# Three small attentions issued in groups of two or three pairs of tiles, with a group's products in one row

## The chip, the cores and the metric

The program runs on one core of a Trainium2 chip. A core has five engines that run their own instruction streams side by side and meet at semaphores: the matrix engine (TensorE, PE in the profile; its weight loads are shown as PEld), the vector engine (VectorE, DVE), the scalar engine (ScalarE, ACT), GpSimd (POOL) and SyncE (SP). Data moves between memory and the core's buffer by DMA transfers that an engine's queue issues. Matmul results land in eight accumulation banks of 128 partitions by 512 f32 values.

The metric is the time of one execution of the whole program in device microseconds (us).

## The reference

The reference is a residual network of sixteen layers over x of shape (16, 256, 128), in f32: each layer adds its output for the normed x to x. The order is: a linear attention with a running error, a local attention, a performer attention, the local attention again, a linear attention with a convolution, a layer of eight experts of which two are taken for each token, a decay attention, the experts again, a causal linear attention, a channel mix, a window attention with its own experts, the mix again, a rotary attention, an adapter layer of experts, a state-space layer and the adapters again.

The change touches three of them, each with 16 heads of 8 dimensions over 256 tokens. Cut to what they compute:

```python
def decay(x):                     # every pair of tokens
    scores = einsum('bqhd,bkhd->bhqk', q, k) * 8**-0.5
    scores = scores * exp(-alpha * abs(i - j))
    return einsum('bhqk,bkhd->bqhd', softmax(scores), v) @ Wo.T + bo

def causal_linear(x):             # key not after query, no softmax
    q, k = relu(q) + 1e-6, relu(k) + 1e-6
    out = einsum('bhnd,bhnde->bhne', q, cumsum(einsum('bhnd,bhne->bhnde', k, v)))
    return (out / max(scale * position, 1e-6)) @ proj.T

def rope(x):                      # key not after query
    q, k = rotate(q), rotate(k)   # real halves kept, the others set to 0
    scores = where(causal, q @ k.T * 8**-0.5, -1e10)
    return (softmax(scores) @ v) @ Wo.T + bo

x = x + layer(layernorm(x))       # sixteen times
```

## The kernel before, in words

x stays on the core as 128 channels by 4096 tokens, cut into 8 chunks of 512 tokens. A chunk holds two sequences (b = 0, 1), and a sequence has two tiles of 128 tokens. A pair of tiles is (it, jt): query tile and key tile. The softmax is taken without subtracting a maximum; `guard` records the largest entries of queries and keys, and another program is run in the end if they are too large.

The three stages `decay` (L2905), `rope` (L2978) and `causal_linear` (L3025) give their own parts to one shared routine, `small_stage` (L2766). Each names its pairs in `units`: decay has four per sequence ((0,0) and (1,1) with a decay table, (0,1) and (1,0) with a decay that is folded into queries and keys beforehand as `qx` and `kx`), causal_linear two ((0,0) and (1,1); the pair between them is carried by a sum over the first tile), rope three ((0,0), (1,0) and (1,1)). An item is one pair of one sequence of one chunk; decay has 64 items, eight a chunk, causal_linear 32, rope 48.

An item's work on PE has two parts, and the array is cut differently for them:

- `score(n)` (L2783): four row-tiled matmuls (32 rows each; the masked queries of four heads side by side as moving data) into four banks. They are evicted into a score buffer `pt` of 128 by 2048 f32: in decay by four table multiplies on DVE, then an exp over the whole buffer on ACT in the next slot; in decay's other kind and in rope by four exps on ACT, for rope's diagonal pairs then a mask on DVE in the next slot; in causal_linear by masks on DVE and copies on ACT with masks on POOL.
- `weigh_by_head` (L2818; decay and rope) or `weigh` (L2797; causal_linear): 16 column-tiled products (32 columns each, 128 by 128) into one bank.

Everything else on PE uses the whole array: the norm of the chunk (`norm_x_step`, three steps), the projections, the values, and after the last product of a query tile in decay and rope `raw` (a copy out of the bank: by ACT for tile 0, by DVE for tile 1), `turn` (L2839: four transposes and a division by the sum), `join` (L2854: two transposes back and a copy into `ot`), `out` (L2865: the output projection, added to x). In causal_linear `finish` takes the place of raw, turn and join. After `out` come the steps that lead into the next layer (`lead`, L1831): for causal_linear and rope the next norm, where it is taken over; for decay the eight steps of the sending to the experts: three of the norm, `compare` (the router's matmul and a comparison, on PE, DVE and POOL), `choose` (DVE, POOL), `place`, `turn` (transposes, two copies on ACT) and `scatter` (L3620), which issues eight indirect DMAs from POOL's queue. The expert stage's first fetch waits for the last scatter.

The order of all of this is written out by hand: under `manual_schedule` each engine gets its instructions in the order in which the Python code issues them. The loop goes over slots n, one item a slot. In a slot it issues the score of item n, then what is due in this slot (the rest of the last eviction, lead steps, turn, join), then an output projection if one is ready, then the products of item n − 3 (`lag = 3`), then the steps of `steps` whose offset falls on this slot. An offset counts slots from the chunk's first score: (−6, project) is six slots ahead of it. `masked_copy` (L2894) makes the masked queries `qz` by two DVE and two ACT operations. Eight banks are split into six for scores and whole-array work and two for products; there are four `pt` buffers.

Helpers that record instructions, so that many operations share a line: `mm` L503, `tr` (transposes) L507, `act` L527, `tt` (DVE) L530, `gt` (POOL) L533, `ts` L537 and L539, `stt` L542, `copy_out` L638.

Of the kernel before, what the change touches and what calls it, by code (L numbers as in the profile page):

```python
# [11 lines left out]
F32, BF16, I32 = mybir.dt.float32, mybir.dt.bfloat16, mybir.dt.int32  # L12
# [1636 lines left out]
class Fast(Net):  # L1649
# [1116 lines left out]
    def small_stage(self, w, units, steps, tiles, evict, finish=None):  # L2766

        nc = self.nc
        lag = 3
        with ExitStack() as st:
            p = self.stage(st, "sm", 1)
            items = [(c, b, *u) for c in range(NCH) for b in range(2) for u in units]
            pts, po, ots, os, later, due = {}, {}, {}, {}, [], {}
            lead = self.lead(p, "s")
            first = min(at for at, _ in steps) - 4  # L2780
            steps = [(first + i, lambda c, i=i: self.norm_x_step(p, c, i, "s")) for i in range(3)] + list(steps)

            def score(n):  # L2783
                c, b, it, jt, kind = items[n]
                k, q, _ = tiles(c, b, it, jt)
                pt = p.tile([P, 4, 4, P], F32, tag="pt", name="pt", bufs=4)
                ps = []
                for r in range(4):
                    rows = slice(32 * r, 32 * r + 32)
                    ps.append(self.bank("s"))  # L2790
                    self.mm(ps[r].rearrange("p (h t) -> p h t", h=4), k[rows], q[rows])
                rest = evict(kind, pt, ps)
                if rest:
                    due.setdefault(n + 1, []).append((lambda _: rest(), None))
                pts[n] = pt

            def weigh(n):  # L2797
                c, b, it, jt, kind = items[n]
                vz = tiles(c, b, it, jt)[2]
                if n % len(units) == 0:  # L2800
                    po[0] = self.bank("o")
                pt = pts.pop(n)
                first, last = n % len(units) == 0, n % len(units) == len(units) - 1
                for u in range(4):
                    for r in range(4):
                        cc = slice(32 * r, 32 * r + 32)
                        nc.tensor.matmul(
                            po[0][cc, it * P : it * P + P], vz[:, u, cc], pt[:, r, u], start=first and u == 0,
                            stop=last and u == 3, skip_group_check=True,
                        )  # L2810
                if last:
                    if b == 0:
                        ots[c] = p.tile([P, CH], F32, tag="ot", name="ot", bufs=2)
                    finish(c, b, ots[c][:, b * T : b * T + T], po[0])
                    if b == 1:
                        later.append(c)

            def weigh_by_head(n, slot):  # L2818
                c, b, it, jt, kind = items[n]
                vo = tiles(c, b, it, jt)[2]  # L2820
                mine = [i for i, u in enumerate(units) if u[0] == it]
                first, last = n % len(units) == mine[0], n % len(units) == mine[-1]
                if first:
                    po[it] = self.bank("o")
                pt = pts.pop(n)
                for u in range(4):
                    for r in range(4):
                        nc.tensor.matmul(
                            po[it][32 * r : 32 * r + 32, u * P : u * P + P], vo[:, 4 * r + u], pt[:, r, u],
                            start=first and u == 0, stop=last and u == 3, skip_group_check=True,  # L2830
                        )
                if last:
                    raw = p.tile([P, CH], F32, tag="raw", name="raw", bufs=2)
                    self.copy_out(it, raw, po.pop(it))
                    due.setdefault(slot + 1, []).append((lambda n: turn(n, raw), n))
                    if it:
                        due.setdefault(slot + 2, []).append((join, n))

            def turn(n, raw):  # L2839
                c, b, it, *_ = items[n]  # L2840
                pt = self.bank("s")
                for u in range(4):
                    self.tr(pt[:, u * P : u * P + P], raw[:, u * P : u * P + P])
                src = pt.rearrange("p (u r d) -> p u r d", u=4, r=4)
                rd = p.tile([P, 4, 4], F32, tag="rd", name="rd", bufs=2)
                nc.vector.reciprocal(rd, src[:, :, :, 8])
                o = p.tile([P, P], F32, tag="o", name="o", bufs=3)
                self.tt(
                    o.rearrange("p (r u d) -> p u r d", r=4, u=4), src[:, :, :, :8],
                    rd[:, :, :, None].broadcast_to([P, 4, 4, 8]), ALU.mult,  # L2850
                )
                os[c, b, it] = o

            def join(n):  # L2854
                c, b, *_ = items[n]
                if b == 0:
                    ots[c] = p.tile([P, CH], F32, tag="ot", name="ot", bufs=2)
                pt = self.bank("s")
                for it in range(2):
                    self.tr(pt[:, it * P : it * P + P], os.pop((c, b, it)))  # L2860
                self.act(ots[c][:, b * T : b * T + T], pt[:, :T], AF.Copy)
                if b == 1:
                    later.append(c)

            def out(c):  # L2865
                pz = self.bank("s")
                self.mm(pz, w["Wo"], ots.pop(c))
                x = self.x[:, self.chunk(c)]
                if "bo" in w:
                    self.stt(x, pz, w["bo"], x, ALU.add, ALU.add)  # L2870
                else:
                    self.tt(x, x, pz, ALU.add)

            with self.share(s=6, o=2), self.tc.manual_schedule():
                self.logs()
                many = 2 * len(units)
                for n in range(first, len(items) + lag + (1 if finish else 3) + len(lead)):
                    if 0 <= n < len(items):
                        score(n)
                    for f, c in due.pop(n, []):  # L2880
                        f(c)
                    if later:
                        c = later.pop()
                        out(c)
                        for i, f in enumerate(lead):
                            due.setdefault(n + 1 + i, []).insert(0, (f, c))
                    if lag <= n < len(items) + lag:
                        weigh(n - lag) if finish else weigh_by_head(n - lag, n)
                    for at, f in steps:
                        c, u = divmod(n - at, many)  # L2890
                        if u == 0 and 0 <= c < NCH:
                            f(c)

    def masked_copy(self, pool, q, b):  # L2894

# [9 lines left out]
    def decay(self, w):  # L2905
# [4 lines left out]
        with ExitStack() as st:  # L2910
# [34 lines left out]
            def queries(c, b):  # L2945
                qzs[c, b] = self.masked_copy(p1, qs[c], b)
# [5 lines left out]
            def queries_by_edge(c, b):  # L2952
                qxs[c, b] = p1.tile([P, 4, T], F32, tag="qx", name="qx", bufs=3)
                self.gt(qxs[c, b], qzs[c, b], edge[:, None, :].broadcast_to([P, 4, T]), ALU.mult)
# [7 lines left out]
            def tiles(c, b, it, jt):  # L2962
# [2 lines left out]
                return kk[c][:, j : j + P], qq[c, b][:, :, it * P : it * P + P], vzs[c % 2][:, 2 * b + jt]  # L2965

            steps = [
                (1, guard), (-6, project), (-5, values), (-4, lambda c: queries(c, 0)), (-3, keys_by_edge),
                (-2, lambda c: queries_by_edge(c, 0)), (0, lambda c: queries(c, 1)), (2, lambda c: queries_by_edge(c, 1)),
            ]  # L2970
            units = [(0, 0, 0), (0, 1, 1), (1, 1, 0), (1, 0, 1)]
            self.small_stage(w, units, steps, tiles, evict)
# [5 lines left out]
    def rope(self, w):  # L2978
        h0 = self.ha
        nc = self.nc  # L2980
        with ExitStack() as st:
# [28 lines left out]
            def queries(c, b):  # L3010
                qzs[c, b] = self.masked_copy(p1, held[c, "q"], b)

            def tiles(c, b, it, jt):
# [1 line left out]
                return held[c, "k"][:, j : j + P], qzs[c, b][:, :, it * P : it * P + P], vzs[c % 2][:, 2 * b + jt]  # L3015

            steps = [
                (0, lambda c: self.guard(ROPE, c, held[c, "q"], held[c, "k"])),
                (-5, lambda c: turned(c, "q")), (-4, lambda c: turned(c, "k")), (-2, values),
                (-3, lambda c: queries(c, 0)), (-1, lambda c: queries(c, 1)),  # L3020
            ]
            units = [(0, 0, 1), (1, 0, 0), (1, 1, 1)]
            self.small_stage(w, units, steps, tiles, evict)
# [1 line left out]
    def causal_linear(self, w):  # L3025
# [3 lines left out]
        with ExitStack() as st:  # L3029
# [46 lines left out]
            def queries(c, b):  # L3076
                qzs[c, b] = self.masked_copy(p1, qs[c], b)
# [24 lines left out]
            def finish(c, b, o, po):  # L3102
# [3 lines left out]
                self.gt(o[:, P:], cross, rd[:, P:], ALU.mult)  # L3106

            steps = [
                (-5, project), (-4, first_tiles), (-3, lambda c: queries(c, 0)), (-2, values),
                (-2, summed), (-1, lambda c: queries(c, 1)), (0, crossed),  # L3110
            ]
            self.small_stage(w, [(0, 0, 0), (1, 1, 0)], steps, tiles, evict, finish)

# [609 lines left out]
```

## Time and profile before

| | us |
|---|---|
| median of 3 runs | 4578.29 |
| lowest and highest | 4572.87, 4580.91 |
| the profiled execution's own time | 4623.81 |
| its span on the core | 4621.7 |
| PE busy (share of the span) | 4064.9 (88%) |
| DVE busy | 2502.5 (54%) |
| ACT busy | 2349.6 (51%) |
| POOL busy | 1946.4 (42%) |

The granted clock of TensorE is 0.943 of full speed over the span. The profile is one execution and stands 45.5 us above the median of the timed runs. In it the decay stage lies at 2315 to 2632 us from the start, causal_linear at 2858 to 2992, rope at 4003 to 4223. Lines of a timeline give the start, the duration, the engine, the line of the kernel, the operation, the tile written and the tile read; "32*128" is a row-tiled, "128*32" a column-tiled and "128*128" a whole-array matmul; x8 means that eight such instructions were put together. What stands in brackets is the idle time before, with what ended it.

### The profile page before, as it was taken

What the parts mean: (1) busy time and instruction counts of PE and PEld (TensorE: products, weight loads), DVE (VectorE), ACT (ScalarE), POOL (GpSimd) and SP (SyncE); (2) the same over time, 40 slices, a digit from 0 to 9 for tenths busy, and PEclk for the clock granted to TensorE, in tenths of its full rate; (3) what the DMA queues carried; (4) which work ended last, traced back from release to release, by engine and by line L of the source; (5) the groups of instructions that cost most, each with busy time, mean ns of one, the idle gap of its engine ahead of it and who ended that gap; (6) DMA issues with size and microseconds to landing.
All of it is one profiled execution on the core that took longest, in us unless ns stands there. A gap on an engine that the chain in (4) does not pass through costs nothing. (4 is left out here: it accounts for less than half of the span.)

```text
span 4621.7 us, 71773 instructions
## 1 busy us (share of the span) xinstructions
PE 4064.9 (88%) x28232; PEld 2185.1 (47%) x28232; DVE 2502.5 (54%) x4453; ACT 2349.6 (51%) x4425; POOL 1946.4 (42%) x1784
## 2 busy tenths in 40 slices
PE   6899999999899999957988698979998888898868
PEld 2455455574455455436744386533333333444323
DVE  4764665462665576462365434635656566476454
ACT  6665465446665466532376433454444443664432
POOL 4653454232654354144434344644433366421241
PEclk9999999999999999978999799989999989999979
DMA  1800000000000000015400162000000000000000
GB/s 55 317 1 1 10 1 1 18 1 1 19 1 1 3 2 1 1 32 173 142 7 15 58 194 78 18 15 1 1 1 1 3 1 0 14 1 17 6 0 19
DMA packets 73081, 142.36 MB, mean 31 GB/s; under 512 B 11007, under 2 KB 42373, under 8 KB 72609
## 3 DMA queue, kind: packets, MB, share of 16 engines
q1 hardware_dynamic: 57120, 114.46, 7.5%
q0 software_dynamic: 9088, 16.94, 1.1%
q10 hardware_dynamic: 6528, 6.29, 0.4%
q8 instruction: 226, 3.70, 0.3%
q14 instruction: 119, 0.97, 0.1%
HBM read 84.22 MB, written 55.25 MB: 30 GB/s over the span
## 5 line engine op out<-in xcount | busy, mean ns | idle before, releaser
L527 ACT ACTIVATE pt<-ps 128x512 f32<-128x512 f32 (+1 forms) x896 | 420.2, 537 | 300.4 <-PE ps L503 296.3
L503 PE MATMUL ps<-hb,w 128*128 128x512 f32 (+1 forms) x960 | 482.4, 630 | 27.7 <-DVE hb L542 21.6
L503 PE MATMUL ps<-w,hb 128*128 128x512 f32 (+2 forms) x896 | 416.0, 578 | 18.7 <-DVE t L530 11.6
L530 DVE TENSOR_TENSOR t<-ps,tab 128x512 f32<-128x512 f32 x512 | 319.2, 683 | 195.9 <-ACT sq L527 192.1
L533 POOL TENSOR_TENSOR t<-t,ss 128x1024 f32<-128x1024 f32 x128 | 243.5, 1902 | 312.4 <-ACT ss L527 203.6
L533 POOL TENSOR_TENSOR t<-t,t 128x512 f32<-128x512 f32 x256 | 320.1, 1272 | 13.1 <-PE ps L503 10.1
L503 PEld LDWEIGHTS ps<-hb,w 128*128 128x128 f32 (+1 forms) x960 | 180.5, 197 | 306.5 <-issue 245.8
L533 POOL TENSOR_TENSOR nsq<-ha 128x512 f32<-128x512 f32 x128 | 141.8, 1108 | 362.2 <-ACT ha L527 338.9
L503 PE MATMUL ps<-nsq,ct 128*128 128x512 f32 x368 | 214.8, 668 | 80.3 <-POOL nsq L533 62.2
L530 DVE TENSOR_TENSOR u<-u,ps 128x512 f32<-128x512 f32 x220 | 129.2, 591 | 227.8 <-PE ps L503 157.2
L527 ACT ACTIVATE pt<-pt 128x768 f32<-128x768 f32 (+1 forms) x160 | 170.1, 1063 | 156.3 <-DVE pt L530 156.3
L503 PE MATMUL ps<-ot,w 128*128 128x512 f32 x448 | 211.1, 607 | 28.5 <-ACT ot L527 21.8
L2182 POOL DMA_INDIRECT back<-y,x x156 | 152.5, 978 | 198.0 <-ACT y L527 169.3
L530 DVE TENSOR_TENSOR ot<-ps,rd 128x512 f32<-128x512 f32 (+1 forms) x208 | 136.3, 655 | 177.4 <-ACT rd L527 142.0
L503 PE MATMUL ps<-qkt 64*128 64x192 f32 (+1 forms) x2048 | 217.3, 328 | 11.8 <-ACT pt L527 11.8
L503 PE MATMUL ps<-u,w 128*128 128x512 f32 (+1 forms) x448 | 221.7, 618 | 5.9 <-POOL u L533 5.9
L503 PE MATMUL ps<-xt,w 128*128 128x256 f32 x936 | 220.4, 386 | 3.6 <-DMA w<-in_moe_x 2.6
L503 PEld LDWEIGHTS ps<-qkt 64*128 64x128 f32 x2048 | 154.2, 189 | 135.6 <-ACT qkt L527 51.5
L503 PEld LDWEIGHTS ps<-w,hb 128*128 128x128 f32 x896 | 148.1, 193 | 143.3 <-issue 103.0
L527 ACT ACTIVATE nrs<-ps,ct 128x512 f32<-128x512 f32 x208 | 140.1, 685 | 146.1 <-PE ps L503 143.2
L530 DVE TENSOR_TENSOR pt<-ps,w 128x384 f32<-128x384 f32 (+1 forms) x320 | 171.1, 575 | 76.0 <-PE ps L503 72.6
L527 ACT ACTIVATE rd<-rd 128x256 f32<-128x256 f32 x256 | 106.7, 417 | 207.6 <-DVE rd L530 201.4
(359 smaller groups left out, 8840.4 us busy)
## 6 DMA issues: line engine op xcount, KB each, us to landing
w<-in_moe_x SPq DMA_DIRECT2D x78, 533.0 KB
rows<-t SPq DMA_DIRECT2D x64, 520.0 KB
x<-rows SPq DMA_DIRECT2D x78, 130.0 KB
w<-in_local_f SPq DMA_DIRECT2D x8, 659.5 KB
y<-back ACTq DMA_DIRECT2D x16, 256.0 KB
y<-back SPq DMA_DIRECT2D x16, 256.0 KB
w<-in_local_f SPq DMA_DIRECT2D x4, 658.5 KB
back<-y,x POOLq DMA_INDIRECT x156
```

The costliest lines, as they stand in the source:

```text
L503: self.nc.tensor.matmul(out, lhsT, rhs, start=start, stop=stop)
L527: self.nc.scalar.activation(out, in_, func, **kw)
L530: self.nc.vector.tensor_tensor(out, a, b, op)
L533: self.nc.gpsimd.tensor_tensor(out, a, b, op)
L2182: nc.gpsimd.indirect_dma_start(views[2 * i + t], bass.IndirectOffsetOnAxis(ap=x[:, t, C : C + 1].bitcast(I32), axis=0), y[:, t], None, bou ...
```

## The change

- A group is two slots where the number of pairs is even (decay, causal_linear) and three in rope.
- The products of a group's items are no longer issued one a slot, three slots behind the score. They are all issued in the last slot of the next group, one after the other, behind that slot's score.
- Due work no longer goes into any slot: `later` puts it into slots that are not the last of their group (with groups of two, every second slot). Turn comes one such slot after the products, join two, out three (causal_linear: out one), and the lead steps in the slots after that, one in each. The three norm steps stand a group apart.
- What is due in a slot is issued in reverse order of its entry; the rest of the eviction comes first, the stage's own steps come ahead of the products instead of behind them.
- Score buffers: 2 × group, four as before in decay and causal_linear, six in rope.
- Offsets of the stages' own steps move so that they fall on slots that are not the last of a group; in decay keys_by_edge goes from −3 to −2, beside queries_by_edge of sequence 0.

```diff
-        lag = 3
+        many = 2 * len(units)
+        group = 2 if len(units) % 2 == 0 else 3
...
-            first = min(at for at, _ in steps) - 4
-            steps = [(first + i, lambda c, i=i: self.norm_x_step(p, c, i, "s")) for i in range(3)] + list(steps)
+            first = min(at for at, _ in steps) - 3 * group
+            steps = [(first + i * group, lambda c, i=i: self.norm_x_step(p, c, i, "s")) for i in range(3)] + list(steps)
+
+            def later(n, i, f, c):
+
+                for _ in range(i):
+                    n += 1 if n % group < group - 2 else group - n % group
+                due.setdefault(n, []).append((f, c))
...
-                pt = p.tile([P, 4, 4, P], F32, tag="pt", name="pt", bufs=4)
+                pt = p.tile([P, 4, 4, P], F32, tag="pt", name="pt", bufs=2 * group)
...
-                rest = evict(kind, pt, ps)
-                if rest:
-                    due.setdefault(n + 1, []).append((lambda _: rest(), None))
+                rests[n] = evict(kind, pt, ps)
...
-                        later.append(c)
+                        later(slot, 1, out, (slot, c))
...
-                    due.setdefault(slot + 1, []).append((lambda n: turn(n, raw), n))
+                    later(slot, 1, lambda n: turn(n, raw), n)
                     if it:
-                        due.setdefault(slot + 2, []).append((join, n))
+                        later(slot, 2, join, (slot, n))
...
-                    later.append(c)
+                    later(slot, 3, out, (slot, c))
...
+                for i, f in enumerate(lead):
+                    later(slot, (2 if finish else 4) + i, f, c)
...
-                many = 2 * len(units)
-                for n in range(first, len(items) + lag + (1 if finish else 3) + len(lead)):
+                n = first
+                while n < len(items) + group or due:
                     if 0 <= n < len(items):
                         score(n)
-                    for f, c in due.pop(n, []):
+                    if rest := rests.pop(n - 1, None):
+                        rest()
+                    for f, c in reversed(due.pop(n, [])):
                         f(c)
-                    if later:
-                        c = later.pop()
-                        out(c)
-                        for i, f in enumerate(lead):
-                            due.setdefault(n + 1 + i, []).insert(0, (f, c))
-                    if lag <= n < len(items) + lag:
-                        weigh(n - lag) if finish else weigh_by_head(n - lag, n)
                     for at, f in steps:
                         c, u = divmod(n - at, many)
                         if u == 0 and 0 <= c < NCH:
                             f(c)
+                    if n % group == group - 1:
+                        for i in range(n - 2 * group + 1, n - group + 1):
+                            if 0 <= i < len(items):
+                                weigh(i, n) if finish else weigh_by_head(i, n)
+                    n += 1
...
             steps = [
-                (1, guard), (-6, project), (-5, values), (-4, lambda c: queries(c, 0)), (-3, keys_by_edge),
-                (-2, lambda c: queries_by_edge(c, 0)), (0, lambda c: queries(c, 1)), (2, lambda c: queries_by_edge(c, 1)),
+                (-6, project), (-4, values), (-4, lambda c: queries(c, 0)), (-2, keys_by_edge),
+                (-2, lambda c: queries_by_edge(c, 0)), (0, lambda c: queries(c, 1)), (0, guard), (2, lambda c: queries_by_edge(c, 1)),
             ]
...
             steps = [
-                (0, lambda c: self.guard(ROPE, c, held[c, "q"], held[c, "k"])),
-                (-5, lambda c: turned(c, "q")), (-4, lambda c: turned(c, "k")), (-2, values),
-                (-3, lambda c: queries(c, 0)), (-1, lambda c: queries(c, 1)),
+                (-6, lambda c: turned(c, "q")), (-5, lambda c: turned(c, "k")), (-3, values), (-2, lambda c: queries(c, 0)),
+                (0, lambda c: queries(c, 1)), (1, lambda c: self.guard(ROPE, c, held[c, "q"], held[c, "k"])),
             ]
...
             steps = [
-                (-5, project), (-4, first_tiles), (-3, lambda c: queries(c, 0)), (-2, values),
-                (-2, summed), (-1, lambda c: queries(c, 1)), (0, crossed),
+                (-6, project), (-4, first_tiles), (-4, lambda c: queries(c, 0)), (-2, values),
+                (-2, summed), (0, lambda c: queries(c, 1)), (0, crossed),
             ]
```

## The prediction

> **What bounds the kernel now.** I read the view by stretches of time first, over the three stages that the change touches (decay, causal_linear, rope, in this order), then over single chunks of them, from one output projection to the next. Columns: the stretch and its length, busy time (instructions) of PE, PEld, DVE, ACT and POOL, the granted clock, the DMA share, GB/s.
>
> ```profile
> 2315.00:2632.00 317.00, 259.07 (x3028) 140.23 (x3026) 178.47 (x447) 193.80 (x306) 116.10 (x110) 0.90 0.05 15
> 2858.00:2992.00 134.00, 129.36 (x1531) 70.89 (x1532) 97.71 (x208) 68.43 (x138) 87.55 (x90) 0.99 0.01 2
> 4003.00:4223.00 220.00, 196.99 (x2245) 103.91 (x2246) 159.44 (x212) 137.84 (x281) 48.86 (x27) 0.96 0.01 1
> 2344.58:2371.66 27.08, 26.59 (x362) 14.09 (x358) 17.50 (x35) 21.17 (x34) 6.00 (x3) 1.00 0.01 2
> 2407.34:2447.12 39.78, 32.50 (x387) 17.68 (x383) 21.70 (x55) 24.81 (x40) 15.44 (x15) 0.91 0.05 15
> 2900.37:2918.87 18.50, 18.26 (x199) 9.66 (x199) 12.81 (x28) 10.22 (x20) 12.32 (x13) 1.00 0.00 1
> 4099.12:4127.80 28.68, 26.25 (x287) 13.15 (x287) 21.05 (x28) 18.86 (x38) 8.69 (x5) 1.00 0.01 1
> ```
>
> The three stages are 671 of 4621.7 us. PE is the fullest engine in each: causal_linear's chunk is PE alone (18.26 of 18.50); rope leaves 2.4 us of 28.68; decay's first chunks are full (26.59 of 27.08), but from the third on, where the sending to the experts (scatters) runs beside the attention, a chunk takes 40 us with 7 idle.
>
> Next the timeline of PE in causal_linear: start, length, line, operation, array tile. Row groups (32*128) are scores, column groups (128*32) products, 128*128 whole-array work.
>
> ```profile
> 2851.55 1.88 PE L503 MATMUL ps<-ha,w 128*128 128x512 f32 x4
> 2853.27 0.94 PE L503 MATMUL ps<-w,ha 128*128 128x128 f32 x7
> ...
> 2912.12 1.14 PE L503 MATMUL ps<-qz,k 32*128 32x512 f32 x8
> 2913.19 1.13 PE L503 MATMUL ps<-nsq,ct 128*128 128x512 f32 x2
> 2914.24 1.08 PE L2807 MATMUL ps<-pt,vz 128*32 128x128 f32 x32
> 2915.25 1.14 PE L503 MATMUL ps<-qz,k 32*128 32x512 f32 x8
> 2916.32 1.08 PE L2807 MATMUL ps<-pt,vz 128*32 128x128 f32 x32
> 2917.34 0.94 PE L503 MATMUL ps<-w,ha 128*128 128x128 f32 x6
> ```
>
> Two projections of 512 columns in one mode start 1.72 us apart, 0.86 each. The same work takes 1.07, 1.05, 1.01, 1.07, 1.02 start to start where the mode changes. So a change costs: rows to whole 0.21, whole to columns 0.19, columns to rows 0.15, rows to columns 0.21, columns to whole 0.16; 0.18 on average.
>
> Then decay's fifth chunk on POOL and PE, the place of the idle time:
>
> ```profile
> 2504.92 1.06 POOL L3624 DMA_INDIRECT rows<-out,idx  x1 [5.27 <-ACT out L527]
> 2506.28 0.96 POOL L3624 DMA_INDIRECT rows<-out,idx  x1 [0.30 <-issue]
> ...
> 2513.85 0.96 POOL L3624 DMA_INDIRECT rows<-out,idx  x1 [0.30 <-issue]
> 2514.83 1.27 POOL L533 TENSOR_TENSOR kx<-k,edge 128x512 f32<-128x512 f32 x1
> ...
> 2526.64 2.36 POOL L533 TENSOR_TENSOR qx<-qz,edge 128x1024 f32<-128x1024 f32 x1
> ```
> ```profile
> 2517.05 1.12 PE L507 MATMUL ps<-ct,raw 128*128 128x128 f32 x4 [5.70 <-ACT raw L527]
> 2518.10 1.94 PE L2828 MATMUL ps<-pt,vo 128*32 128x128 f32 x32
> 2519.97 1.84 PE L503 MATMUL ps<-qz,k 32*128 32x512 f32 x8
> ```
> ```profile
> ACT raw L527 <- remote: 43.7, 5, 9.4
> ```
>
> A chunk's eight scatters hold POOL's queue from 2504.92 to 2514.81, 1.26 us apart, and kx stands right behind them. While they run, ACT's copy `raw` waits for something that no engine of the core released ("remote" in the list of waits, 5 times, up to 9.4 us), although PE had finished its products; PE's transposes then wait 5.70, and the next products take 1.87 start to start for 1.01, the scores 1.77 for 1.07.
>
> I take this withheld signal to belong to the profiling. PE's finished signals are late in this way by 4.5, 6.8, 6.8, 7.1, 7.2 and 4.5 us in decay, by 3.3 and 6.5 in the stage before it: 46.7 us, and the profiled execution (4623.81) is 45.5 above the median (4578.29). So my accounts are of an execution without it: a loaded decay chunk then takes 40.5 less 5.7 of waiting and about 2 of slow work, some 32.7 us. The sum is put on the median; for a profiled execution the same sum starts at 4623.81.
>
> **The change part by part.**
> *Mode changes.* Decay has 26 a chunk, 4.7 us at 0.18. After it, each of its four groups goes scores, whole, scores, columns: 0.21 + whole to rows (taken as 0.2) + 0.21 + 0.15, 3.1 in all: 1.6 saved. Causal_linear: 14 (2.5 us) against two such groups (1.5): 1.0 saved. Rope, groups of three with whole-array work in two slots: about 19.4 changes counted in the timeline (3.5) against 2 × 1.18: 1.1 saved. Over eight chunks 13 + 8 + 9 = 30 us, if PE sets the pace everywhere. The number of matmuls stays.
>
> *causal_linear.* PE does set it. Against the 1.0: the group's second score needs four of six banks just after the first, and out now comes one group after finish, whose last multiply (0.45) stands on POOL behind two masks of 1.15. I take 0.4 for both, so −0.6 a chunk, −5 us. Ends: −8 (all of it kept), +3 (0.4 more a chunk than saved).
>
> *rope.* Out's wait for `ot` goes too, since join is now followed by a whole-array slot before out: it is 1.6 to 2.1 us in each chunk, as here, slow clock behind it.
>
> ```profile
> 4127.80 1.12 PE L503 MATMUL ps<-ot,w 128*128 128x512 f32 x2 [1.83 <-ACT ot L527]
> 4130.52 2.08 PE L503 MATMUL ps<-nsq,ct 128*128 128x512 f32 x2
> ```
>
> That is 2.9 off 28.5. What is late next is ACT: three scores come closer together, each with an eviction of 2.05 us against 0.86 of matmul, and six banks hold one score and a half. I take half back: −1.4 a chunk, −11. Ends: −23 and 0.
>
> *decay, pace.* 1.6 saved. But a group's last products are now followed by one score and then the transposes; `raw` of the first query tile is copied by ACT, behind an eviction (2.05) and a whole exp (1.95). PE has one score, 1.07, to fill it: about 1.4 of waiting, in some of the two places a chunk. Net nothing; ends −13 (all saved) and +10 (both waits in full, 2.8 a chunk).
>
> *decay, POOL's queue.* Scatter was issued four slots behind a chunk's end, kx three slots ahead of the next, qx two: the second score, which needs both, was five slots (some 20 us) behind scatter's start. Now scatter, kx and qx all stand at slot 6 of eight, in this order, and behind the next sending's `ahead`; score 1 of the next chunk comes three slots later, 3/8 of 32.7 = 12.3 us. POOL from the start of slot 6: `ahead` done at about 6.4 (it waits for DVE, behind an eviction of 2.48 and the router's steps), scatters 8 × 1.26 to 16.5, kx 1.27 to 17.8, qx 2.36 to 20.1. PE waits 7.8, with the group's products queued behind that score, and then loses 0.86 + 0.70 = 1.6 at the slow clock. 9.4 a time. Scatter of chunks 0 to 3 meets the scores of chunks 4 to 7: four times, +38. Ends: 4 × 2.4 = +10 (`ahead` done at 1) and +50 (3 us later).
>
> One rule is weighed here. The Trainium skill, TensorE: Matmul & The Clock Gate, Part 1, says the array's clock is halved after an idle activity window and stays so for about 3.4 us. By it a stall costs an estimated 1.7 beside the wait, and the four 38 as by the row.
>
> *decay, tail.* A sending's eight steps go into every second slot. The last output stands at 2615.35, the last scatter ends at 2642.8, 27.4 later, and the next stage's first fetch waits for it. Now scatter 6 stands between the last chunk's router steps on POOL, not ahead of them: about 8 of its 10.1 us are added. Ends 0 and +12.
>
> *Everything else*: norm steps spread out, queries a slot or two earlier or later, guard (two DVE operations of 0.68): in a chunk where DVE has some 11 and ACT 8 of 32.7 us free; nothing, ±3. More score buffers (2 MB at most) cost no instruction.
>
> Sum: −5 − 11 + 0 + 38 + 8 = +30: 4608 us.
>
> A rule against the change: TensorEngine Tiling (Array Packing), PSUM Bottleneck, says that tiling speeds the matmuls but not the emptying of their banks. The rows agree for decay (2.48 and 2.05 an eviction). Taken for rope too, it would leave +41 in place of +30.
>
> **The rivals.**
> 1. *Faster: POOL is in time.* Without the 38 the sum is −8; with the better ends of causal_linear, rope and decay and no tail −44; the middle is −26: 4552. It decides if kx and qx are done 12.3 us after slot 6 starts. For it: POOL has 24 of 40 us free. Against: 13.7 us of POOL work in the order written there, already more than 12.3 without any wait.
> 2. *The withheld signal is no artefact* but in every execution. Then a loaded chunk is 40.5, and POOL's wait falls partly where PE waits anyway: decay +2 × 4 and tail +8, the other two −16: 0, 4578. Against: the difference of 45.5.
> 3. *Changes of mode are not the pace* in decay and rope, since ACT and DVE are, and the queue costs little: −5 + 8: 4581, the same. in a loaded decay chunk PE has 32.50, ACT 24.81; in rope's PE 26.25, DVE 21.05. Bursts alone would have to do it.
> 4. *Worse*: both waits for `raw` in full in every decay chunk (+10) and POOL 3 us later (+12) besides: 4630.
>
> **How the numbers follow.** POOL's wait 0.55 (4592 to 4632), faster 0.18, the signal withheld in every execution 0.12, no effect 0.10, worse 0.05. 0.2% of 4578 is 9 us, about what a measurement can tell from no change: 4569 to 4587. Rivals 2 and 3 lie mostly within it: same 0.15, with 0.06 of them above; slower 0.66, faster 0.19. The range leaves out half of the faster case and the top: 4554 to 4634.
>
> **What would show it.** PE in each stage: scores, whole, scores, products twice (or thrice) without a change. Causal_linear's chunk 17.6 to 18.1; rope's some 27, out without 1.8 us for `ot`. In decay, four waits of PE or its weight loads on POOL `qx`, of some 8 us, a chunk apart, kx and qx right behind eight indirect DMAs; the last scatter 33 to 37 us behind the last output. I am wrong if qx is ready before its score, if `ahead` stands behind the scatters or if they start earlier than 6 us into slot 6.

## The result and the profile after

The changed kernel takes 4630.88 us (median of 4 runs, 4613.84 to 4637.9) against 4579.43 (4 runs, 4572.87 to 4580.91): a ratio of 1.011, 95% interval 1.008 to 1.0139. It is slower by 51.5 us. The forecast was slower, 4608, with a range of 4554 to 4634. Its profiled execution took 4637.9 us, span 4636.1.

The kernel before itself takes 4573 to 4584 us in the first comparison and in the last four experiments, and 4613 to 4633 (42 runs) on the chip of the first eight, so every experiment is compared with the kernel before on its own chip.

By stretches of time, with the columns of the prediction: a decay chunk with scatters, an early one without, two chunks of causal_linear, one of rope. These stretches go from one output projection to the next. In the prediction's rows that holds for rope alone; its stretches of decay and causal_linear go from one score to the score a chunk later, which is also a chunk's length.

```profile
2475.60:2516.90 41.30, 32.92 (x384) 19.32 (x383) 26.66 (x57) 25.18 (x41) 16.24 (x15) 0.88 0.04 14
2373.60:2402.00 28.40, 26.68 (x361) 15.22 (x360) 17.23 (x36) 21.91 (x35) 2.38 (x1) 1.00 0.01 2
2913.00:2936.20 23.20, 20.50 (x198) 11.98 (x198) 14.12 (x27) 10.19 (x20) 12.36 (x13) 0.92 0.00 1
2936.20:2959.40 23.20, 20.60 (x199) 11.51 (x199) 13.64 (x27) 10.29 (x20) 12.41 (x13) 0.93 0.01 2
4111.70:4136.40 24.70, 24.70 (x288) 14.09 (x287) 21.14 (x29) 18.85 (x39) 5.32 (x4) 1.00 0.01 2
```

Rope's chunk went from 28.68 to 24.70, with PE busy in all of it. Causal_linear's went the wrong way, from 18.50 with PE full to 23.20 with 2.7 us idle and a lower granted clock (0.92 for 1.00). Decay's loaded chunk, one beside which scatters run, is 41.30.

In decay the waits of PE, from the list of waits (engine, tile, line, releaser: sum, times, longest), and the timelines of PE and POOL around one of them:

```profile
PE ps L507 <- ACT raw L527: 23.9, 14, 3.5
PE ps L503 <- POOL qx L533: 20.7, 4, 6.7
```
```profile
2481.82 2.06 PE L503 MATMUL ps<-qz,k 32*128 32x512 f32 x8
2486.02 1.11 PE L507 MATMUL ps<-ct,raw 128*128 128x128 f32 x4 [2.14 <-ACT raw L527]
...
2493.89 2.16 PE L503 MATMUL ps<-qx,kx 32*128 32x512 f32 x8 [4.79 <-POOL qx L533]
2495.97 3.42 PE L2834 MATMUL ps<-pt,vo 128*32 128x128 f32 x64
```
```profile
2479.47 0.72 POOL L533 TENSOR_TENSOR ahead<-ahead,ct 128x256 f32<-128x256 f32 x1 [7.33 <-DVE ahead L530]
2480.34 1.06 POOL L3633 DMA_INDIRECT rows<-out,idx  x1 [0.16 <-POOL ahead L533]
...
2489.29 0.96 POOL L3633 DMA_INDIRECT rows<-out,idx  x1 [0.31 <-issue]
2490.27 1.27 POOL L533 TENSOR_TENSOR kx<-k,edge 128x512 f32<-128x512 f32 x1
2491.49 2.34 POOL L533 TENSOR_TENSOR qx<-qz,edge 128x1024 f32<-128x1024 f32 x1
```

This is the new wait that was forecast: `ahead`, eight scatters, kx, qx on POOL's queue, and PE standing four times for qx with 64 products behind it, which then run slower (3.42 us for the 1.95 they take at the full clock).

In causal_linear PE stands before the output projection:

```profile
2936.22 2.07 PE L503 MATMUL ps<-ot,w 128*128 128x512 f32 x2 [1.43 <-POOL ot L533]
```

The prediction had put this wait and the shortage of banks at 0.4 us a chunk together. This record and a second one of the same kernel (after_again, below) also differ by 12 us in the window attention, which the change does not touch; so what each stage is worth is taken from kernels run beside each other, not from subtracting two records.

### The profile page after: what moved, and what is told of

It is laid out like the page before. It is cut to its first block, busy times and chain, and to the rows that moved or that the text cites. A ratio compares the mean times of both kernels' runs of the same rounds, so it can differ in the third digit from the quotient of the medians.

```text
span 4636.1 us, 71820 instructions
## 1 busy us (share of the span) xinstructions
PE 4083.9 (88%) x28232; PEld 2223.3 (48%) x28232; DVE 2516.7 (54%) x4453; ACT 2351.5 (51%) x4425; POOL 1933.5 (42%) x1784
## 5 line engine op out<-in xcount | busy, mean ns | idle before, releaser
L503 PE MATMUL ps<-w,hb 128*128 128x512 f32 (+2 forms) x896 | 418.4, 581 | 17.8 <-DVE t L530 10.0
L533 POOL TENSOR_TENSOR t<-t,t 128x512 f32<-128x512 f32 x256 | 320.1, 1272 | 13.1 <-PE ps L503 10.1
L503 PEld LDWEIGHTS ps<-qkt 64*128 64x128 f32 x2048 | 153.5, 189 | 135.3 <-ACT qkt L527 51.5
L530 DVE TENSOR_TENSOR pt<-pt,w 128x1024 f32<-128x1024 f32 (+1 forms) x96 | 156.4, 1629 | 105.0 <-ACT pt L527 105.0
```

Of the source, the lines that this page charges most:

```text
L503: self.nc.tensor.matmul(out, lhsT, rhs, start=start, stop=stop)
L530: self.nc.vector.tensor_tensor(out, a, b, op)
L533: self.nc.gpsimd.tensor_tensor(out, a, b, op)
```

## The experiments

### One stage at a time

The edit leaves the old routine in place and gives the new one, under another name, to one stage with that stage's new offsets.

```diff
 class Fast:
     def small_stage(...)          # as before
+    def small_stage_grouped(...)  # as changed
...
-            self.small_stage(w, units, steps, tiles, evict)
+            self.small_stage_grouped(w, units, steps, tiles, evict)
```

> Groups in decay alone, causal_linear and rope as before. Theory A (the signal that PE's finish withheld during the scatters in the profile of before is not in its timed runs, and in the grouped order PE waits for qx behind the scatters four times): the loss is about 38 for the four waits and up to 8 for the tail, 4615 to 4626 us. Theory B (the withheld signal is in every execution): by the two profiles decay is about 1 us longer, 4577 to 4585.

> Groups in causal_linear alone. By the profiles its chunk went from 18.5 to 23.2 us and the stage is some 31 us longer: 4605 to 4613 us. The prediction had this stage 5 us shorter, 4574.

> Groups in rope alone. By the profiles its chunk went from 28.5 to 24.5 us and the stage is some 25 to 30 us shorter: 4548 to 4556. The prediction had 11 us: 4568.

Measured, with the kernel before at 4620.55 (20 runs): decay alone 4632.38, ratio 1.0027 (1.0017 to 1.0037); causal_linear alone 4645.24, 1.0049 (1.0037 to 1.0061); rope alone 4595.10, 0.9946 (0.9933 to 0.9959). In microseconds +12, +25, −25. So the prediction's sign for causal_linear is refuted, and its size for rope.

Decay's +12 fell between the two theories, because a premise of both was wrong. In the records of these three the signals of PE are late in decay, as in the profile shown of before, and the kernel before takes 41 us more in all its runs here than in the first comparison. So the lateness is not made by the profiling: it goes with the longer times here. In the record of the changed kernel from the first comparison no engine waits for a signal of this kind.

### The whole change, and the scatters behind kx and qx

The changed kernel was run again here; and a version of it that issues the scatters of a slot after the stage's own steps:

```diff
+                    behind = []
                     for f, c in reversed(due.pop(n, [])):
-                        f(c)
+                        if len(lead) == 8 and f is lead[7]:
+                            behind.append((f, c))
+                        else:
+                            f(c)
                     for at, f in steps:
...
+                    for f, c in behind:
+                        f(c)
```

> The changed kernel once more, beside the others on one chip. If the kernel before stands near 4579 here, as in the first comparison, the loss is some 50 us; if it stands near 4620, as beside the single stages, the sum of those three (+12, +25, -25) is +11: about 4632 either way.

> The changed kernel, but in decay the eight scatters of a slot are issued behind that slot's own steps, so that kx and qx of the next chunk stand ahead of them on POOL's queue; nothing else is moved. Theory A: the four waits for qx (20.7 us in the profile after, and some 8 to 10 us of slow clock behind them) go, 4600 to 4606 us. Rival: the time is set by the waits for raw and by ACT, and the wait only moves to the next late thing (the second sequence's qx, now behind the scatters): 4622 to 4632.

The changed kernel took 4633.17 against 4622.45 (22 runs): 1.0025 (1.0015 to 1.0034), or +10.7 us, where the three single stages add up to +11. It takes about the same as in the first comparison (4630.88); it is the kernel before that differs. With the scatters behind, 4627.80 against 4620.55: 1.0013 (1.0003 to 1.0023), some 4 us nearer to before. That lies in the rival's range, though the intervals of the two kernels overlap. On this chip the waits of the changed kernel are these (the recorded execution took 4615.10):

```profile
PE ps L507 <- ACT raw L527: 35.4, 12, 7.1
...
PE ps L503 <- POOL qx L533: 3.9, 1, 3.9
```
```profile
2473.84 2.11 PE L503 MATMUL ps<-qz,k 32*128 32x512 f32 x8
2482.76 1.11 PE L507 MATMUL ps<-ct,raw 128*128 128x128 f32 x4 [6.81 <-ACT raw L527]
2483.67 1.91 PE L503 MATMUL ps<-x,ct 128*128 128x512 f32 x2
2485.37 0.63 PE L507 MATMUL ps<-ct,o 128*128 128x128 f32 x2
2485.94 1.31 PE L503 MATMUL ps<-qx,kx 32*128 32x512 f32 x8
```

PE already stands for `raw` while the scatters run (its signal to ACT is late), and when it comes to the score that needs qx, qx is done. The two waits lie on top of each other, and the chunk comes out as long as in the first record: 41.34 us from output to output for 41.30.

The record with the scatters behind looks different:

```profile
PE ps L507 <- ACT raw L527: 24.5, 13, 5.6
PE ps L2834 <- issue: 11.4, 18, 1.1
```

The waits for qx are gone, and so, but for one of 2.0 us, are the late signals, although this is the same chip. In their place PE stands 11.4 us in 18 pieces inside its own products while the scatters run, with nothing in the profile that it waits for ("issue"). The four loaded chunks take 158.0 us in place of 162.6, about what the times of the two kernels differ by. So taking the wait for qx away did not uncover the wait for `raw`; something else took its place, and what that is was not found.

### What causal_linear waits for

In the record of causal_linear alone PE waits for `ot` eight times. DVE, for its part, stands once a chunk before its copy of the new keys, and only then evicts the scores that were issued meanwhile:

```profile
PE ps L503 <- POOL ot L533: 9.9, 8, 1.6
DVE k L539 <- PE ps L503: 22.3, 5, 4.5
```
```profile
2922.96 0.69 DVE L539 TENSOR_SCALAR q<-ps 128x512 f32<-128x512 f32 x1 [1.89 <-PE ps L503]
2928.12 0.69 DVE L539 TENSOR_SCALAR k<-ps 128x512 f32<-128x512 f32 x1 [4.46 <-PE ps L503]
2928.72 0.88 DVE L2744 COPY vz<-ps 128x128 f32<-128x128 f32 x4
```

PE had projected the keys at 2923.6. What DVE waits for is the score that still reads the buffer (two for k): project was moved from five to six slots ahead of its chunk, past the score in slot −5. Behind that copy stand the score's own evictions. Two edits, on causal_linear alone: the projection and what follows it one group later,

```diff
-                        later(slot, 1, out, (slot, c))
+                        later(slot, 2, out, (slot, c))
...
-                    later(slot, (2 if finish else 4) + i, f, c)
+                    later(slot, (3 if finish else 4) + i, f, c)
```

and a third buffer for q and k:

```diff
-                    held[c] = p2.tile([P, CH], F32, tag=n, name=n)
+                    held[c] = p2.tile([P, CH], F32, tag=n, name=n, bufs=3)
```

The third kernel has both, with rope grouped as well and decay as before.

> Groups in causal_linear alone, with the output projection and the steps after it one group later. Theory C (the stage's 25 us are the projection's wait of 1.44 us a chunk for ot on POOL, and the wait of DVE's copy of k for the score that still reads the buffer, which holds back that score's own evictions): 8 times 1.4 to 2, so 11 to 16 us less than with groups alone, some 9 to 14 us above before. Theory D (the bunched whole-array work empties too slowly whatever its order): still 20 to 25 us above before.

> Groups in causal_linear alone, with three buffers for q and k in place of two. Theory C: DVE's k no longer waits 4.5 us, the score behind it loses its 1.9 us, so 8 to 15 us less than with groups alone: 10 to 17 us above before. Theory D: 20 to 25 us above before.

> Groups in rope and causal_linear, with the later output projection and three q and k buffers in causal_linear; decay as before. Theory C: causal_linear comes out between 0 and 8 us below before (fewer changes of mode, 1.0 a chunk, less what the third late thing takes), rope 25 below: 25 to 33 us below before. Theory D: causal_linear still 15 or more above: 10 us or less below before.

Measured against 4622.45: out later 4628.80, 1.0012 (1.0003 to 1.0021), so the loss of 25 us fell to 6; three buffers 4636.42, 1.0033 (1.0021 to 1.0045), to 14; both with rope 4589.23, 0.9931 (0.9918 to 0.9945), 33 us faster than before, 8 beyond what rope alone gave. Theory C holds, by each edit alone and by both; the later projection saved 18 us where 11 to 16 were expected. Each edit takes away its own wait and leaves the other, as the lists of waits show, first with the later projection, then with three buffers:

```profile
PE ps L503 <- POOL ot L533: 0.9, 1, 0.9
```
```profile
PE ps L503 <- POOL ot L533: 9.8, 8, 1.6
DVE k L539 <- PE ps L503: 0.8, 5, 0.2
```

With the later projection DVE still waits 26.9 us before k. From output to output a chunk is 21.60 us with groups alone, 19.15 with the first edit, 19.70 with the second. In the third kernel rope's chunk is 24.70, as in the changed one, and a chunk of causal_linear this:

```profile
2905.70:2922.80 17.10, 17.10 (x202) 10.09 (x198) 13.56 (x27) 10.08 (x20) 11.79 (x13) 1.00 0.01 2
```

17.10 with no idle time, against 18.50 with 0.24 idle before. PE changes its mode 8 times in this chunk, 14 times before. So with the two waits gone the chunk is 1.4 us shorter, somewhat more than the 1.0 that was worked out for the changes. This kernel is faster than both the kernel before and the changed one.

### What decay waits for, with and without scatters

To see a chunk without scatters beside one with them, the scatters of the even chunks are kept and issued with those of the next odd chunk, sixteen in a row; all rows are still sent. A second form puts eight multiplies on POOL where the even chunks' scatters were; their product is used by nothing. They were meant to be as long as the scatters; in the record they hold POOL for 8.9 us, eight scatters for 10.1.

```diff
         def scatter(c):
             idx, out = held.pop(c)
+            if late and c % 2 == 0:
+                kept.append((c, idx, out))
+                for k in range(8):       # the second form only
+                    net.gt(still, out[:, k % 2, :, :C], out[:, k % 2, :, :C], ALU.mult)
+                return
+            for c, idx, out in kept + [(c, idx, out)]:
+                send(c, idx, out)
+            kept.clear()
```

> The kernel before, but in decay the scatters of the even chunks are kept and issued with those of the next odd chunk (16 in a row); everything is still sent. Theory A (the idle time of a loaded chunk is PE's signal withheld while scatters run): the stretch between the outputs of chunks 3 and 4, now without scatters, takes 32 to 34 us in place of 40.3. Theory B (a loaded chunk is that long from its own work on ACT and DVE): 39 to 41 us.

> As before_pair, with eight multiplies of 1.27 us on POOL where the even chunks' scatters were (their products are thrown away), so POOL is held as long but nothing is transferred. Theory A: as before_pair within 1 us, since in the old order kx and qx have 7 us to spare: 32 to 34 us between the outputs of chunks 3 and 4.

> Groups in decay alone, scatters in pairs of chunks as in before_pair. The stretch between the outputs of chunks 4 and 5 has no scatters. Theory A: 32 to 35 us in place of 40 to 41 (pace of the old order within 1.3 us, no wait for qx). Theory B: 39 to 41 us.

> As grouped_pair, with the eight multiplies on POOL where the even chunks' scatters were. Theory A (POOL's queue alone makes PE wait for qx, whatever fills it): between the outputs of chunks 4 and 5, PE waits 5 to 8 us for qx and the stretch takes 6 to 10 us more than in grouped_pair, 40 to 43. Rival (the wait for qx comes from the scatters' transfers): as grouped_pair.

These four ran on a chip where the kernel before takes 4579.19 (9 runs, 4575.37 to 4583.59), and none of their records has the late signals. The totals are 4603.33 (1.0053, 1.0038 to 1.0067), 4607.52 (1.0059, 1.0042 to 1.0075), 4657.87 (1.0172, 1.0155 to 1.0189) and 4666.49 (1.0191, 1.0174 to 1.0208); they hold the cost of sixteen scatters in a row and of a later last scatter, so the reading is from the chunks. Two of the old order, from before_pair:

```profile
2456.90:2489.70 32.80, 31.03 (x382) 17.05 (x382) 22.24 (x57) 25.09 (x40) 12.64 (x12) 1.00 0.04 12
2419.20:2456.90 37.70, 33.22 (x383) 17.55 (x383) 22.91 (x57) 25.20 (x40) 19.19 (x18) 0.95 0.07 21
```

The first was meant to be without scatters, but the next row of sixteen begins 7 us before its end: six of them lie in it (hence the 12 GB/s), and the second holds nine of the row before. So the first shows six scatters without a late signal, in 32.8 us, where the prediction had taken 32.7 for a loaded chunk with no late signal; a chunk with just its own eight was not recorded. In the second PE waits 2.35 us for `nsq`, a step of the norm, which stands behind the scatters on POOL. With POOL held by the multiplies the first chunk is 32.80 again: in the old order POOL has time to spare for eight. In groups, without any scatter, and with POOL held:

```profile
2513.70:2548.30 34.60, 31.00 (x383) 17.94 (x382) 22.43 (x57) 24.78 (x40) 7.46 (x6) 0.90 0.01 2
```
```profile
2518.20:2557.50 39.30, 30.86 (x382) 18.19 (x381) 26.10 (x57) 24.68 (x40) 15.70 (x14) 0.91 0.01 1
...
2535.17 2.16 PE L503 MATMUL ps<-qx,kx 32*128 32x512 f32 x8 [4.84 <-POOL qx L533]
```

39.30 against 34.60, with PE waiting 4.84 us for qx while no scatter is issued: it is the place in POOL's queue that costs, not the transfers. The wait is a little under the 5 to 8 us that were expected, and the chunk 4.7 longer for 6 to 10. The chunks with sixteen scatters in the grouped order say the same in another way. PE's waits for qx in grouped_pair:

```profile
PE ps L503 <- POOL qx L533: 31.1, 2, 16.0
```

15.6 us each, against 20.7 / 4 = 5.2 with eight scatters: 10.4 us more for eight more scatters of 1.26 us (10.1). The wait grows with the queue nearly one for one.

## Why the prediction was right, and where it was wrong

**Right: decay's wait on POOL, in place and in kind.** Worked out from the start of slot 6: scatters to 16.5 us, kx to 17.8, qx to 20.1. In the record, from that slot's score at 2474.04: 16.2, 17.5 and 19.8. Four times, as forecast. The size was too large: 9.4 a time was taken. The wait is 5.2 on average, and a chunk with scatters is 41.30 against 34.60 without, 6.7 in all (the other three 6.9, 5.7 and 4.8). The term that was mis-sized is the time in which PE comes to the score: 3/8 of a chunk, 12.3 us, was taken; PE came at 2489.1, 15.1 us after the start, because on the way it waited 2.14 for `raw`, and two of its scores took 2.06 and 1.69 us for 1.14 at a granted clock of 1.00 (their weight loads wait for DVE and ACT). So 24 for the 38 over the four chunks.

**Right: the tail.** +8 was taken. The last scatter ends 36.1 us after the last output, for 27.4 before: +8.7. What this costs the whole program was not measured by itself.

**Open: decay's pace.** Net nothing was taken, with +10 as the end at which both waits for `raw` are paid. The lists of waits of before_pair and grouped_pair:

```profile
PE ps L507 <- ACT raw L527: 7.4, 6, 1.3
```
```profile
PE ps L507 <- ACT raw L527: 22.4, 13, 3.5
```

The 22.4 us are both waits in full (2.8 a chunk). Since the old order has 7.4 of them too, 15 are added, against the 13 that the fewer changes of mode could save: about +2. The two chunks that can be set side by side, 34.6 for 32.8, would give +14 if all eight were like them, and an early chunk is shorter in groups (28.40 for 30.55 in before, with less of the sending in it). So the term lies between +2 and +14.

**Right for the first comparison, wrong in its reason: the late signals.** The step "I take this withheld signal to belong to the profiling" was wrong, since on the chip of the first eight experiments the kernel before takes 4613 to 4633 in every run. It still gave a fair account of the kernel before in the first comparison (32.8 measured for 32.7, with six scatters). The sum of 46.7 that stood for it owed something to chance: 9.8 of it are waits in the stage before decay, where the records of before and before_pair keep together (their first outputs in decay stand at 2360.13 and 2358.09). From there to the last output before takes 255.2 us and before_pair 220.0. That the late signals are the 41 us between the two times of the kernel before (4620.55 and 4579.19) is argued from this, not shown: it was not recorded, as it stands, at the lower of them. Rival 2, put down as the signal withheld in every execution, is what happens on that chip: the whole change costs 11 us there, not 51. The changed kernel's loaded chunks are as long in both records, because its wait for qx falls into the time of the late signal; the kernel before stands an estimated 7.5 us a chunk longer (40.3 for 32.8).

**Wrong: causal_linear.** "I take 0.4 for both, so −0.6 a chunk, −5 us" became +25, outside its ends of −8 and +3. Both things were named, and both were under-priced. The output's wait for `ot` is 1.44 a chunk: `ot` stands on POOL behind two masks of 1.07, and the one score between products and projection covers only a part; with the projection later, 18 of the 25 us are gone. The bank shortage was seen as a shortage of banks; it is made by DVE's copy of k waiting 4.46 us for a buffer, with the evictions queued behind it; a third buffer takes 11 of the 25 us away. This is the item that the working on moved steps should have asked of project: who still reads the buffer that it writes, and what stands behind it on its engine. With both mended the stage gains some 8 us (33 less rope's 25; this stage was not run alone with both), as the idea of the change has it.

**Wrong in size: rope.** "I take half back: −1.4 a chunk, −11"; measured −25, beyond the better end of −23. The term that was mis-sized is what ACT takes back, and hardly any of it shows: PE has no wait in 24.70 us, and only one of its scores is held up, for 2.47 us, where one took 2.04 before. Of the 4.0 us of the chunk shown, 1.83 are the wait for `ot`, as worked out; 0.61 are a wait for `nsq` on POOL, which the prediction did not have; the other 1.55 are busy time of PE, for which the changes of mode had been put at 1.1. The slow clock behind the wait for `ot` is no part of these 4.0, since the granted clock is 1.00 in that chunk before and after. It is in the next chunk of before, 30.31 us long:

```profile
4108.02 1.12 PE L503 MATMUL ps<-nsq,ct 128*128 128x512 f32 x2 [0.61 <-POOL nsq L533]
```
```profile
4127.80:4158.11 30.31, 27.88 (x286) 14.04 (x286) 21.05 (x28) 18.86 (x38) 8.68 (x5) 0.94 0.01 2
```

There the two matmuls that the prediction showed (4130.52) take 2.08 us, and 1.13 in the chunk shown. This account of rope is read from its rows; no edit took its waits away one by one.

**The sum.** +30 against +51.5: causal_linear was 30 too low, rope 14 too high. What is left of the 51.5 for decay is an estimate of 39 to 52, for the 46 taken: rope's −25 is taken out, and causal_linear as the +25 of its runs or as +38 (eight chunks of 23.2 for 18.5, as in the record after). Within decay POOL's wait was 14 too high and the pace up to 14 too low. So the forecast of slower stands on its own mechanism, the wait on POOL, and the nearness of the total owes something to errors of opposite sign.

On the clock, the Trainium skill, TensorE: Matmul & The Clock Gate, Part 1, says that the activity window runs free, so that the same kernel meets the slow clock differently from run to run. The two records of the changed kernel agree: the projection behind a wait of 1.43 us takes 2.07 us in the record after, at a granted clock of 0.50, and 1.12 behind the same wait in after_again; that chunk of causal_linear is 23.2 us in the one and 21.6 in the other.

## What to carry to other kernels

Putting matmuls of one array mode in a row paid 1.4 us in causal_linear's chunk of 18.5 and, with the waits that went too, 4.0 in rope's of 28.7, but only where nothing that PE needs next was put later than the grouped order can wait for. When steps are moved in an order written by hand, go through each queue: who still reads the buffer that a moved step writes, what now stands ahead of it on its engine (eight scatters are 10 us of POOL), and how many slots are left to the first reader. Price such a wait by the queue's own sum of durations, since it grew nearly one for one, and take off what the waiting engine is late by itself.

## What was not expected

PE's finished signals came 4.5 to 8 us late while the eight scatters ran, in seven of the eight records from one chip, in the old order and in the grouped one alike; in the record after and in the four from the other chip they were on time. In that time ACT and DVE waited for products that PE had finished. The kernel before differs by 41 us between the two chips (4620.55 and 4579.19). In the eighth record of the first chip, where kx and qx stand ahead of the scatters, the late signals are all but gone and PE stops inside its own products. What holds the signals back was not found, and whether it belongs to the chip or to something that goes with it was not tried.
